# Query-key products of a causal attention regrouped by four PSUM banks and alternated between row halves

## The chip, the core and the metric

The kernel runs on one core of one Trainium2 chip. The metric is device time in microseconds (us) of that core; before the change the median of three runs was 1920.82 us (1916.88 to 1924.34). A core has engines with queues of their own that run side by side and wait for each other by semaphores: TensorE (PE: matrix products; its weight loads are listed apart as PEld), VectorE (DVE), ScalarE (ACT), GpSimd (POOL), and SyncE (SP), which here issues the DMAs. Products land in PSUM, which here is handed out in eight banks of 128 partitions x 512 fp32 values; VectorE and ScalarE read them from there.

## What is computed

One block of a hybrid model, on x of 4 x 256 x 512: attention with a rotary embedding and a small adapter prefix, a clustered feed-forward layer, a state-space mixer, and the feed-forward layer again, each added to x behind a layer norm. The change touches the attention alone:

```python
qkv = jnp.einsum('btc,oc->bto', x, w_attn)
...
q = _apply_rope(q, cos, sin)
k = _apply_rope(k, cos, sin)
scores = jnp.einsum('bhqd,bhkd->bhqk', q, k) / jnp.sqrt(jnp.asarray(hd, x.dtype))
causal = jnp.tril(jnp.ones((T, T), bool))
scores = jnp.where(causal, scores, jnp.asarray(-jnp.inf, x.dtype))
attn = jax.nn.softmax(scores, axis=-1)
y = jnp.einsum('bhqk,bhkd->bhqd', attn, v)
```

There are 32 heads of 16 values, 256 tokens in each of four sequences. Queries 0 to 127 can see keys 0 to 127 only; queries 128 to 255 see up to all 256.

## The kernel before, in words

`attention` goes through 32 units: four sequences of eight, a unit being four heads (`i` in the loop at L608). The steps of a unit are spread over four turns of that loop: `scores` of unit i, `turn` of unit i-1, `weigh` of i-2, `gathered` of i-3. Beside them run jobs in slices: `prepared` (norm and projections of the next sequence), `pieces` (rotated queries and keys stacked and transposed), `adapter_scores`, `adapted`, `ended` (output projection) and, in the last eight units, `fed` (feed-forward tiles).

The stacks made by `pieces` hold each head in 64 rows: the high and low parts of 16 values, in an order that makes one product of 64 rows the high-precision product of queries and keys. Two heads lie above each other in 128 partitions, so a head's product uses one half of TensorE's rows, `rows = slice(64 * pr, 64 * pr + 64)`.

`scores` (L413) works with four banks a unit: c is the block of 128 queries, pr the row half. For each bank it issues two products (L425, j = 0 and 1, always against all 256 keys), then a product of the identity with a mask (L429, all 128 rows, bf16), which adds -1e30 above the diagonal. VectorE takes the negative maximum (L434), ScalarE two exponentials with their sums (L437), one for each head in the bank; then the bank is free. `turn` (L443) transposes the exponentials in three tiles of four transposes (L452), each copied out (L453) by VectorE or ScalarE. `weigh` multiplies with the values (L462, L468), with four heads side by side in column strips of 32.

PSUM in this stage, eight banks: two under the tag "m" for everything general (`trp` L378, `pq` L269, `pa` L387, `pt` and `pya` in `adapted`, `try`, `po`, `pd`, `tr`), three for scores ("sc"), two for `turn` ("pt"), one for `weigh` ("py"). The projections of the first sequence (L359) and the last two feed-forward tiles (L660) borrow the score banks.

The order within each engine's queue isn't that of the source. A planner simulates the program, takes earlier instructions first but passes over those whose data or bank isn't ready, and fixes each queue before the run. In the queue of TensorE therefore stand transposes, products and pieces of other jobs between the banks of one unit.

## Time and profile before

| | |
|---|---|
| median of three runs | 1920.82 us |
| the profiled execution | 1916.66 us, span 1914.9 us |
| mean granted TensorE clock | 0.990 |
| products of L425 | 256, each 64 rows, 128 x 256 out; half of them for queries 0 to 127 |
| weight loads of L425 (min/median/max) | 182/184/336 ns |
| mask products of L429 | 128, weight loads 94/96/107 ns |
| maxima of L434 | 128, 359/550/693 ns |
| exponentials of L437 | 256, 356/446/534 ns, and as many sums of 185/203/264 ns |
| transposes of L452 | 384, and 96 copies of L453 of 680 (VectorE) or 587 ns (ScalarE) |

The span is the time from the first instruction to the last in one profiled execution; the time of that execution is longer by what lies around it. In lists of instructions the first number is the start in us from the start of the span, the second the length of the group; "x2" is the number merged into the line; the shape reads rows*columns of the weights, then the moving operand. In square brackets stands how long the engine was idle before and what ended the wait. "issue" is a wait that nothing in the profile explains. The ends of products are modelled, so two starts are a better measure of TensorE than one duration.

### The profile page before, as it was taken

The page shows a single profiled execution, that of the slowest core. Times are in us where ns is not written, and L with a number is a line of the kernel's source. Part 1 is how long each engine was busy: PE and PEld are TensorE (multiplying, and loading weights), DVE is VectorE, ACT ScalarE, POOL GpSimd, SP SyncE. Part 2 cuts the span into 40 slices and gives each one's busy share as a digit, 9 for nine tenths or more (in the row PEclk, how much of TensorE's full clock was granted, in tenths as well). Part 3 has the DMA queues.
Part 4 walks back from the last instruction along what each step waited for, and adds up shares of the span by engine and source line. Part 5 has one row for each costly group of instructions (what it writes and reads, how often), then busy time and mean ns, then how long its engine had stood idle before and what let it go on. Part 6 is the DMA issues. An engine that isn't in the chain of part 4 may idle for free.

```text
span 1914.9 us, 29954 instructions
## 1 busy us (share of the span) xinstructions
PE 1866.0 (97%) x10690; PEld 1468.9 (77%) x10690; DVE 1475.2 (77%) x2324; ACT 1383.2 (72%) x2873; POOL 361.0 (19%) x308
## 2 busy tenths in 40 slices
PE   7999999989999999999999999999999999999997
PEld 6767767767777787888787878877777788787786
DVE  5556657678998777877877797778777877877777
ACT  5665667557898677876787787778677877786753
POOL 4212120011331111222111121212111211131100
PEclk7999999989999999999999999999999999999999
DMA  4000000014455554544455454446454554455341
GB/s 141 1 1 1 1 21 24 12 38 155 169 192 184 160 168 140 160 154 160 149 164 161 149 172 156 148 147 187 149 165 154 160 159 160 138 166 162 119 123 49
DMA packets 151909, 240.35 MB, mean 126 GB/s; under 512 B 12368, under 2 KB 77520, under 8 KB 151760
## 3 DMA queue, kind: packets, MB, share of 16 engines
q1 hardware_dynamic: 151760, 238.44, 39.1%
q8 instruction: 84, 1.38, 0.3%
q14 instruction: 65, 0.53, 0.1%
HBM read 202.75 MB, written 35.65 MB: 124 GB/s over the span
## 4 chain that ended last, share of the span: by engine, by line
PE 84%; DVE 6%; ACT 4%; DMA 2%; issue 1%; SPq 0%; DVEq 0%; ACTq 0%
PE pp L112 12%; PE pp L113 11%; PE pp L114 11%; PE pyy L928 8%; PE pog L112 6%; PE pog L114 6%; PE pog L113 6%; PE sc L425 3%; PE trx L913 3%; PE ptr L452 2%; DVE acc L854 2%; PE py L462 1%; PE sc L429 1%; PE trp L380 1%; DMA wor<-in_wout_dram 1%
## 5 line engine op out<-in xcount | busy, mean ns | idle before, releaser
L112 PE MATMUL pp<-mx,w 128*128 128x512 f32 (+1 forms) x1160 | 465.6, 401 | 8.4 <-DVE acc L854 7.9
L114 PE MATMUL pp<-mx,w 128*128 128x512 f32 (+1 forms) x1160 | 454.2, 392 | 0.0
L113 PE MATMUL pp<-mx,w 128*128 128x512 f32 (+1 forms) x1160 | 454.2, 392 | 0.0
L854 DVE SCALAR_TENSOR_TENSOR acc<-pp,cw_s,acc 128x1012 f32<-128x1012 f32 (+2 forms) x240 | 304.8, 1270 | 23.1 <-ACT acc L847 22.4
L902 DVE TENSOR_TENSOR em<-em,gm 128x1536 f32<-128x1536 f32 x128 | 228.4, 1785 | 94.3 <-ACT em L896 86.0
L112 PEld LDWEIGHTS pp<-mx,w 128*128 128x128 f32 x1160 | 218.6, 188 | 66.0 <-issue 9.9
L114 PEld LDWEIGHTS pp<-mx,w 128*128 128x128 f32 x1160 | 218.5, 188 | 45.5 <-issue 0.4
L113 PEld LDWEIGHTS pp<-mx,w 128*128 128x128 f32 x1160 | 218.9, 189 | 40.7 <-issue 0.7
L890 POOL TENSOR_SCALAR_AFFINE_SELECT r<-r 128x512 f32<-128x512 f32 x128 | 144.6, 1129 | 526.6 <-DMA r<-cumd 418.5
L951 POOL TENSOR_TENSOR sq<-sq,acc 128x1024 f32<-128x1024 f32 x55 | 132.6, 2410 | 581.8 <-ACT acc L950 581.8
L104 ACT CAST w<-wr 128x512 fp32r<-128x512 f32 x144 | 88.5, 615 | 187.6 <-PE pp L113 164.4
L112 PE MATMUL pog<-wo,gh 128*128 128x512 f32 x512 | 204.3, 399 | 0.0
L114 PE MATMUL pog<-wo,gh 128*128 128x512 f32 x512 | 200.3, 392 | 0.0
L113 PE MATMUL pog<-wo,gh 128*128 128x512 f32 x512 | 199.9, 390 | 0.0
L895 ACT ACTIVATE em<-r,col_t 128x128 f32<-128x128 f32 x512 | 165.0, 391 | 48.2 <-PE pyy L928 46.5
L928 PE MATMUL pyy<-em,xd 128*64 128x256 f32 (+1 forms) x2048 | 189.1, 330 | 2.4 <-DVE em L902 2.4
L928 PEld LDWEIGHTS pyy<-em,xd 128*64 128x64 f32 x2048 | 134.2, 137 | 63.6 <-issue 21.7
L898 ACT ACTIVATE em<-r,col_t 128x128 f32<-128x128 f32 x512 | 166.5, 389 | 0.0
L886 DVE TENSOR_SCALAR em<-r,col_t 128x128 f32<-128x128 f32 x512 | 137.1, 327 | 12.1 <-PE pyy L928 10.1
L914 DVE TENSOR_TENSOR xd<-trx,dt_t 128x512 f32<-128x512 f32 x128 | 86.2, 683 | 54.6 <-PE trx L913 54.4
L105 DVE TENSOR_TENSOR w<-wr,w 128x512 fp32r<-128x512 f32 x139 | 97.4, 702 | 37.8 <-ACT w L104 37.3
L437 ACT ACTIVATE e<-sc,nmx 128x128 f32<-128x128 f32 (+1 forms) x256 | 105.2, 424 | 15.0 <-DVE nmx L434 14.9
(287 smaller groups left out, 3313.4 us busy)
## 6 DMA issues: line engine op xcount, KB each, us to landing
wr<-in_win_dram SPq DMA_DIRECT2D x287, 256.0 KB, 2.8
r<-cumd SPq DMA_DIRECT2D x128, 512.0 KB, 4.1
spill<-gb SPq DMA_DIRECT2D x63, 512.0 KB, 2.8
gr<-spill SPq DMA_DIRECT2D x120, 256.0 KB, 3.5
wor<-in_wout_dram SPq DMA_DIRECT2D x64, 256.0 KB, 3.1
out_dram<-x SPq DMA_DIRECT2D x8, 256.0 KB, 2.3
x<-in_x_dram SPq DMA_DIRECT2D x1, 1536.0 KB, 10.2
gr<-spill SPq DMA_DIRECT2D x8, 192.0 KB, 2.5
```

The costliest lines, as they stand in the source:

```text
L112: nc.tensor.matmul(o, lh, rh, start=(first and k == 0), stop=False)
L113: nc.tensor.matmul(o, lh, rl, start=False, stop=False)
L114: nc.tensor.matmul(o, ll, rh, start=False, stop=(last and k == n - 1))
L437: nc.scalar.activation(es_[c][:, 2 * j + pr, :], sc[:, j, :n], AF.Exp, bias=nm[:, j : j + 1], accum_out=rs[:, c, h : h + 1],)
L854: nc.vector.scalar_tensor_tensor(av[:, :, d:], pv[:, :, : L - d], cw_s[:, ch, tap : tap + 1], av[:, :, d:], ALU.mult, ALU.add,)
L886: nc.vector.tensor_scalar(e[:, b, 2, :], rv[:, b, 1, :], col_t[:, h, b, 1:2], 0.0, ALU.subtract, ALU.min,)
L890: nc.gpsimd.affine_select(rv[:, :, 0, :], rv[:, :, 0, :], pattern=[[0, B], [1, P]], compare_op=ALU.is_ge, fill=-1e30, base=0, channel_mult ...
L895: nc.scalar.activation(e[:, b, 1, :], rv[:, b, 1, :], AF.Exp, bias=col_t[:, h, b, 2:3])
L898: nc.scalar.activation(e[:, b, 0, :], rv[:, b, 0, :], AF.Exp, bias=col_t[:, h, b, 0:1])
L902: nc.vector.tensor_tensor(e, e, gm, ALU.mult)
L928: nc.tensor.matmul(py[d, b, k * P :], xd[:, 2 * b + k, d], es2[hh][:, b, 2 * k : 2 if k == 0 else 3, :].rearrange("p s i -> p (s i)"), sta ...
L951: (nc.gpsimd if n < NB - 1 else nc.vector).tensor_tensor(sq, sq, x2, ALU.add)
```

## The change

`scores` first issues the products of two banks of one query block in turn, upper half, lower half, upper, lower; the second query block (c = 1) comes before the first. For the first query block only keys 0 to 127 are multiplied (`kT[rows, blk, :n]`), and its tiles are half as wide. After all eight products come, bank by bank, mask, maximum and exponentials. The score pool has four banks; the transposition pool is gone and `turn` takes its tiles from the general pool, which has three.

```diff
-            ps = pool("a_m", 2, space=PSUM)
-            ps_s = pool("a_s", 3, space=PSUM)
-            ps_t = pool("a_t", 2, space=PSUM)
+            ps = pool("a_m", 3, space=PSUM)
+            ps_s = pool("a_s", 4, space=PSUM)
             ps_y = pool("a_y", 1, space=PSUM)
...
-                for c in range(2):
+                made = []
+                for c in (1, 0):
                     n = (c + 1) * P
-                    for pr in range(2):
-                        rows = slice(64 * pr, 64 * pr + 64)
-                        sc = ps_s.tile([P, 2, L], F32, name="sc", tag="sc")
-                        for j in range(2):
-                            blk = (u % 2) * 2 + j
+
+                    pair = [ps_s.tile([P, 2, n], F32, name="sc", tag="sc") for _ in range(2)]
+                    for j in range(2):
+                        blk = (u % 2) * 2 + j
+                        for pr in range(2):
+                            rows = slice(64 * pr, 64 * pr + 64)
                             nc.tensor.matmul(
-                                sc[:, j, :], qT[rows, blk, c * P : (c + 1) * P], kT[rows, blk, :],
-                                start=(j == 0), stop=False,
+                                pair[pr][:, j, :], qT[rows, blk, c * P : (c + 1) * P],
+                                kT[rows, blk, :n], start=(j == 0), stop=False,
                             )
-                        nc.tensor.matmul(
-                            sc[:, :, n - P : n], identb, negb.unsqueeze(1).to_broadcast([P, 2, P]),
-                            start=False, stop=True,
+                    made += [(c, pr, sc) for pr, sc in enumerate(pair)]
+                for c, pr, sc in made:
+                    n = (c + 1) * P
+                    nc.tensor.matmul(
+                        sc[:, :, n - P :], identb, negb.unsqueeze(1).to_broadcast([P, 2, P]),
+                        start=False, stop=True,
+                    )
+                    nm = p3.tile([P, 2], F32, name="nmx", tag="nmx", bufs=4)
+                    nc.vector.tensor_reduce(nm, sc, AX.X, ALU.max, negate=True)
+                    for j in range(2):
+                        h = 4 * u + 2 * j + pr
+                        nc.scalar.activation(
+                            es_[c][:, 2 * j + pr, :], sc[:, j, :], AF.Exp,
+                            bias=nm[:, j : j + 1], accum_out=rs[:, c, h : h + 1],
                         )
...
-                    pt = ps_t.tile([P, 4, P], F32, name="ptr", tag="pt")
+                    pt = ps.tile([P, 4, P], F32, name="ptr", tag="m")
```

The maxima get four small buffers instead of three. What the maxima and exponentials read is as wide as before.

More of the change, by code (lines that the diff above doesn't have):

```diff
@@ L425, in scores @@
                             nc.tensor.matmul(
-                                sc[:, j, :], qT[rows, blk, c * P : (c + 1) * P], kT[rows, blk, :],
-                                start=(j == 0), stop=False,
-                            )
-                        nc.tensor.matmul(
-                            sc[:, :, n - P : n], identb, negb.unsqueeze(1).to_broadcast([P, 2, P]),
-                            start=False, stop=True,
-                        )
-                        nm = p3.tile([P, 2], F32, name="nmx", tag="nmx")
@@ L434, in scores @@
-                        nc.vector.tensor_reduce(nm, sc[:, :, :n], AX.X, ALU.max, negate=True)
-                        for j in range(2):
-                            h = 4 * u + 2 * j + pr
-                            nc.scalar.activation(
-                                es_[c][:, 2 * j + pr, :], sc[:, j, :n], AF.Exp,
-                                bias=nm[:, j : j + 1], accum_out=rs[:, c, h : h + 1],
-                            )
+                                pair[pr][:, j, :], qT[rows, blk, c * P : (c + 1) * P],
```

## The prediction

> **What bounds the kernel now.** I read the engine totals and the 40 slices first, to see which engine is full and where.

> ```profile
> PE 1866.0 (97%) x10690; PEld 1468.9 (77%) x10690; DVE 1475.2 (77%) x2324; ACT 1383.2 (72%) x2873; POOL 361.0 (19%) x308
> ...
> PE   7999999989999999999999999999999999999997
> ...
> PEclk7999999989999999999999999999999999999999
> ```

> TensorE is busy in nearly every slice, at full clock. The changed functions run only in the attention stage, so I cut the trace in three: attention, the passage to the mixer, the mixer.

> ```profile
> core 0: us, PE busy (x) PEld busy (x) DVE busy (x) ACT busy (x) POOL busy (x), PEclk, DMA share, GB/s
> 36.00:370.00 334.00, 331.07 (x2288) 237.51 (x2288) 207.14 (x456) 217.35 (x775) 53.23 (x85) 0.98 0.03 8
> 370.00:440.00 70.00, 57.69 (x319) 47.34 (x318) 51.76 (x114) 36.21 (x60) 9.20 (x8) 0.93 0.15 45
> ```

> In the 334 us of attention VectorE is busy 62%, ScalarE 65%, the DMA engines 3%, TensorE 99%. A busy TensorE may still be stalled, since its ends are modelled; so I ask what waits for what at the line to be changed. TensorE's weight loads there wait 3.3 us in all for ScalarE's exponentials (L437) and 14.0 us for "issue" (64 times, some 0.2 us each), that is, for nothing but TensorE itself. The stage is bound by TensorE's own instruction stream, and time taken out of that stream should come off the span.

> What the stream costs at this place is in the timeline of TensorE alone (start, duration of the merged group, engine, line). Starts matter here, not durations: a product's record lasts some 0.28 to 0.38 us but the next one starts long before.

> ```profile
> 202.29 0.50 PE L425 MATMUL sc<-pc,pc 64*128 64x256 f32 x2
> 202.72 0.28 PE L429 MATMUL sc<-negb,identb 128*128 128x256 bf16 x1
> 202.94 0.50 PE L425 MATMUL sc<-pc,pc 64*128 64x256 f32 x2
> 203.37 0.28 PE L429 MATMUL sc<-negb,identb 128*128 128x256 bf16 x1
> 203.58 0.50 PE L425 MATMUL sc<-pc,pc 64*128 64x256 f32 x2
> 204.01 0.28 PE L429 MATMUL sc<-negb,identb 128*128 128x256 bf16 x1
> 204.13 0.30 PE L397 MATMUL tra<-con,sa 80*128 80x80 f32 x2
> ```

> Two products take 0.43 us until the mask product; the mask takes 0.12 us when a full-height instruction follows (204.01 to 204.13), and 0.21 when a half-height product follows (203.37 to 203.58). So going into half-height work costs 0.09 us. One score bank costs 0.09 + 0.43 + 0.12 = 0.64 us, a unit of four banks 2.57, the 32 units 82 us, a quarter of the stage. What would it cost if nothing were exposed? The nearest row is the adapter's score product, also 256 columns of the same type, but on all 128 rows. In the chain of waits (start, length of the piece):

> ```profile
> 201.51 0.50 PE pa L390 x4
> 202.01 0.35 PE py L468 x6
> 202.36 0.43 PE sc L425 x2
> 202.79 0.21 PE sc L429
> 203.01 0.43 PE sc L425 x2
> 203.44 0.22 PE sc L429
> ```

> Four of those take 0.50 us; start to start their median is 0.118. I use 0.12. Two products would thus need 0.24; the pair takes 0.43, so 0.19 is overhead: the first weight load, which nothing covers, and the emptying before the mask. With the entry, 0.28 us per bank goes to changing between half and full height. The whole chain of the page agrees that this is on the path:

> ```profile
> PE 84%; DVE 6%; ACT 4%; DMA 2%; issue 1%; SPq 0%; DVEq 0%; ACTq 0%
> PE pp L112 12%; PE pp L113 11%; PE pp L114 11%; PE pyy L928 8%; PE pog L112 6%; PE pog L114 6%; PE pog L113 6%; PE sc L425 3%; PE trx L913 3%; PE ptr L452 2%; DVE acc L854 2%; PE py L462 1%; PE sc L429 1%; PE trp L380 1%; DMA wor<-in_wout_dram 1%
> ```

> **The change, part by part.**

> *Grouping.* The eight products of a unit now stand in front of its four masks. If the four banks are free together, there is one entry and one exit instead of four: 0.28 + 8 x 0.12 + 4 x 0.12 = 1.72 us against 2.57, a saving of 0.85 us a unit, 27 us in all. How often are they free together? The order on TensorE is worked out beforehand by a planner that takes what is ready. Today the first three banks of a unit mostly go back to back, as above, and the fourth waits for a free bank. With four banks the same should hold for four. But some units follow within 4 us of each other, while a bank is freed only after its reduce (0.42 or 0.69 us) and two exponentials (starting 0.35 or 0.46 us apart, with their sums), 1.1 to 1.6 us for each bank in turn. Then the two pairs come apart, and each extra entry costs 0.28 us. I take one and a half entries a unit: 0.71 us, 23 us in all.

> *Alternation between the halves.* [...] Loads of 128 columns, one after the other, are 0.11 us each, which is the 0.12 that I already charge. [...]

> [...]

> *First queries take 128 keys, not 256.* Halves the columns of 128 products. At 0.11 us per load, a product of 0.06 us is hidden behind the next load: nothing. The reduce and the exponentials already read only n columns: no change on VectorE or ScalarE (70 and 158 us at these lines).

> *Order: second queries first, and masks later.* VectorE's first reduce of a unit waits for a mask behind up to eight products, 0.5 us later than now. Behind it in its queue stand copies that free transposition banks; VectorE has 38% idle, so it costs nothing unless TensorE is short of such a bank.

> *Banks.* Score banks 3 to 4; the general banks ("m", two) and the transposition banks ("pt", two) become three shared. I count some 210 general tiles and 96 transposition tiles in 334 us, 0.9 a microsecond. Three banks suffice if a tile holds one for 3.3 us on average. A rotated-piece tile holds it about 1.4 us (four transposes, copy of 0.68 or 0.59), a projection 4.3, but an attention transposition some 3, because its four transposes are issued as the exponentials come. That is two banks busy on average, so collisions happen, chiefly while `ended` or `fed` holds two. Bounds: below, a gain of 2 us, since general tiles may now use three banks; above, one exposed round of transposes and copy a unit, 0.44 + 0.68 + some 0.2 of handing over = 1.3 us, 42 us. Nearest row: TensorE's waits in the stage that end with a copy out of a shared or transposition bank (L380 and L452 behind L382, L453, L520; L479 behind L453 and L104; L163) add up to some 4 us. I take as much again: 4 us lost. No DMA is added or moved; what SP issues is the same.

> **Sum.** 23 - 4 = 19 us off. The profiled execution took 1916.66 us (span 1914.9 and 1.8 around it), so 1897.7; it lies 4.2 under the median of 1920.82, so the median should be 1902. What is late next in the stage is still TensorE; ScalarE goes from 65% to 217 / 315 = 69%. The passage behind attention is a chain of VectorE, ScalarE and TensorE steps anchored at attention's end and moves up as a whole.

> **Rivals.**

> *Halves run side by side* and the planner keeps the bursts whole: 27 + 15 - 4 = 38 us off, 1883. For it: concurrent column strips at L462. Against: their staggered loads.

> *The gain is not collected*: TensorE gets ahead and waits for exponentials or banks instead, within 9 us of now, about 1916. For it: each unit needs eight exponentials, 4 x 0.35 + 4 x 0.46 = 3.2 us of ScalarE, before its transposes can end. Against: a third of ScalarE and of VectorE is idle, and three units are in flight.

> *Slower: transposition tiles starve the shared banks.* Each of up to three transposition tiles of a unit holds a bank while it waits for exponentials, and the rotated pieces, adapter products and projections queue behind it on TensorE. At the upper bound of 42 us against 23 that is 19 us slower, 1940; it decides from 0.72 us of added stall a unit. For it: the 3 us holding time and the loss of the separate pool. Against: holdings average two of three. [...]

> **How the numbers follow.** Forecast 0.52, side by side 0.18, not collected 0.14, slower 0.16. A measurement of this kernel tells about 0.5% from no change, 9.6 us: the forecast's own range, 1890 to 1912, is almost all beyond it. Faster 0.70, same 0.15, slower 0.15. The range leaves out the best of the second case and the worst of the fourth: 1881 to 1930.

> **What would show it.** Right: runs of four or eight products with starts 0.11 to 0.12 us apart, one or two entries a unit, the attention stage some 19 us shorter, the mixer unchanged. Side by side: starts in pairs a few ns apart. Wrong: products 0.2 us or more apart within a run, or weight loads of transposes waiting for copies (L453, L382) for tens of microseconds.

## The result, and the profile after

The changed kernel took 1909.45 us (median of 20 runs, 1900.47 to 1923.63), the kernel before 1920.11 (20 runs, 1914.75 to 1924.34). The ratio is 0.9955, with a 95% interval of 0.9937 to 0.9974: some 9 us faster (the medians differ by 10.7), where 19 were forecast. Among all the runs below one stands apart, 5156.97 us in e9 without a known cause, and is left out of ratios and clocks. From the page of the changed kernel, engine totals and granted clock in 40 slices:

```profile
PE 1851.2 (97%) x10690; PEld 1465.2 (77%) x10690; DVE 1475.0 (77%) x2324; ACT 1380.2 (72%) x2873; POOL 352.4 (18%) x308
...
PEclk8999899989999999999999999999999999999999
```

and its three stages, with the same borders as before (busy time of each engine, then the granted clock):

```profile
36.00:370.00 334.00, 321.47 (x2318) 238.40 (x2316) 209.42 (x473) 215.86 (x778) 53.48 (x84) 0.96 0.03 9
370.00:440.00 70.00, 59.02 (x317) 47.81 (x317) 54.03 (x106) 40.62 (x65) 9.20 (x8) 0.93 0.16 52
440.00:1909.00 1469.00, 1444.04 (x7933) 1157.19 (x7931) 1187.56 (x1697) 1106.36 (x1996) 266.88 (x184) 1.00 0.48 155
```

The first pyy product of the mixer starts at 449.3 us instead of 456.6, 7.3 us earlier, and the span ends 6.1 us earlier (1908.8 against 1914.9); so all of the gain lies ahead of the mixer. The chain of waits over the whole span agrees:

```profile
PE 80%; DVE 8%; ACT 6%; DMA 3%; issue 2%; POOL 1%; SPq 0%; DVEq 0%; ACTq 0%; POOLq 0%
PE pp L112 12%; PE pp L113 11%; PE pp L114 11%; PE pyy L932 8%; PE pog L112 6%; PE pog L114 6%; PE pog L113 6%; PE trx L917 3%; DVE acc L858 2%; PE sc L426 1%; DMA wor<-in_wout_dram 1%; PE ptr L456 1%; ACT e L441 1%; PE trp L379 1%; PE py L466 1%
```

The products went from 3% to 1% of the chain, and TensorE from 84% to 80%; VectorE and ScalarE took over most of the difference, the exponentials among them (L441, not in the list before). In the window of attention TensorE isn't full any more (321 of 334 us), and its clock is 0.96 instead of 0.98. The products did become cheaper: added from each start to the next start on TensorE, they take 41.8 us instead of 58.8, while the masks behind them take 21.8 instead of 19.7. Together that is 14.9 us off TensorE's stream, where the forecast had 23. The timeline of TensorE shows both faces of the change, some 3 us apart (start, length of the group, line):

```profile
192.07 0.67 PE L426 MATMUL sc<-pc,pc 64*128 64x256 f32 x8
192.68 0.61 PE L433 MATMUL sc<-negb,identb 128*128 128x256 bf16 x4
...
194.87 0.50 PE L426 MATMUL sc<-pc,pc 64*128 64x256 f32 x2
195.30 0.28 PE L433 MATMUL sc<-negb,identb 128*128 128x256 bf16 x1
195.78 0.50 PE L426 MATMUL sc<-pc,pc 64*128 64x256 f32 x2 [0.20 <-ACT e L441]
...
196.69 0.32 PE L426 MATMUL sc<-pc,pc 64*128 64x128 f32 x1
196.94 0.87 PE L379 MATMUL trp<-con,st 128*128 128x128 f32 x8
197.74 0.32 PE L426 MATMUL sc<-pc,pc 64*128 64x128 f32 x1
198.00 0.53 PE L379 MATMUL trp<-con,st 128*128 128x128 f32 x4
```

At 192.07 a unit has its four banks together: eight products in 0.61 us until the mask; their starts are 0, 3, 221, 224, 339, 342, 397 and 401 ns. They start in pairs 3 or 4 ns apart: the two halves run beside each other. The rows don't name the halves, but the queue of the built kernel does. Of its 46 runs of two products, 15 hold one of each half, and the 14 in the order upper, lower start 3 or 4 ns apart; 31 hold one half only, and those start 162 ns or more apart. At 194.87 the next unit has to take its banks as ScalarE frees them ("<-ACT e L441"), and its products come in twos and ones. Over the stage there are 109 entries from other work into half-height products, against 136 before; runs of eight occur four times. TensorE's weight loads at the products wait 10.0 us for the exponentials, against 3.3. The clock falls behind some of these places. Two of them in the windows view, each row a stretch of 3.4 us or a multiple (length, busy time of the engines, and the clock in the third column from the end):

```profile
191.70:195.20 3.50, 3.26 (x31) 2.63 (x29) 2.13 (x5) 3.00 (x12) 0.92 (x2) 1.00 0.03 7
195.20:198.60 3.40, 3.20 (x23) 2.29 (x21) 2.93 (x6) 3.27 (x16) 0.46 (x1) 1.00 0.01 2
198.60:208.80 10.20, 10.20 (x54) 7.67 (x55) 4.44 (x10) 6.36 (x21) 0.14 (x1) 0.50 0.00 0
208.80:212.20 3.40, 3.26 (x27) 2.07 (x27) 2.17 (x6) 2.31 (x7) 1.50 (x3) 0.99 0.00 0
```

```profile
273.60:277.10 3.50, 3.38 (x34) 2.82 (x32) 1.52 (x4) 3.37 (x9) 1.30 (x3) 1.00 0.00 0
277.10:280.50 3.40, 2.18 (x12) 1.29 (x12) 2.95 (x6) 2.87 (x15) 0.00 (x0) 1.00 0.30 87
280.50:287.30 6.80, 6.80 (x37) 4.76 (x36) 4.63 (x8) 4.58 (x13) 1.24 (x3) 0.50 0.18 52
```

TensorE does 12 instructions between 277.1 and 280.5, among them a wait of 1.02 us for an exponential, and is busy 2.18 of 3.40 us; then it runs 6.8 us at half clock and is "busy" 100% of it, as in the 10.2 us from 198.6. So busy time alone misleads here: of these rows, the two at half clock are the busiest. From the start of the products to 370 us the kernel before has one half-clock stretch, 13.7 us from 35.0 on; the changed one has five, 3.4 us at 34.8, 6.8 at 45.0, 10.2 at 198.6, 6.8 at 280.5 and 3.4 at 355.6, together 30.6.

### The profile page after: what moved, and what is told of

The parts are those of the page before. It is cut to its first block, busy times and chain, and to the rows that moved or that the text cites. A ratio compares the mean times of both kernels' runs of the same rounds, so it can differ in the third digit from the quotient of the medians.

```text
span 1908.8 us, 29962 instructions
## 1 busy us (share of the span) xinstructions
PE 1851.2 (97%) x10690; PEld 1465.2 (77%) x10690; DVE 1475.0 (77%) x2324; ACT 1380.2 (72%) x2873; POOL 352.4 (18%) x308
## 4 chain that ended last, share of the span: by engine, by line
PE 80%; DVE 8%; ACT 6%; DMA 3%; issue 2%; POOL 1%; SPq 0%; DVEq 0%; ACTq 0%; POOLq 0%
PE pp L112 12%; PE pp L113 11%; PE pp L114 11%; PE pyy L932 8%; PE pog L112 6%; PE pog L114 6%; PE pog L113 6%; PE trx L917 3%; DVE acc L858 2%; PE sc L426 1%; DMA wor<-in_wout_dram 1%; PE ptr L456 1%; ACT e L441 1%; PE trp L379 1%; PE py L466 1%
## 5 line engine op out<-in xcount | busy, mean ns | idle before, releaser
L112 PE MATMUL pp<-mx,w 128*128 128x512 f32 (+1 forms) x1160 | 465.2, 401 | 8.7 <-DVE acc L858 8.2
L113 PE MATMUL pp<-mx,w 128*128 128x512 f32 (+1 forms) x1160 | 454.0, 391 | 0.0
L114 PE MATMUL pp<-mx,w 128*128 128x512 f32 (+1 forms) x1160 | 453.9, 391 | 0.0
L112 PEld LDWEIGHTS pp<-mx,w 128*128 128x128 f32 x1160 | 218.3, 188 | 66.4 <-issue 10.0
L114 PEld LDWEIGHTS pp<-mx,w 128*128 128x128 f32 x1160 | 218.6, 188 | 45.5 <-issue 0.4
L113 PEld LDWEIGHTS pp<-mx,w 128*128 128x128 f32 x1160 | 218.8, 189 | 40.7 <-issue 0.7
L894 POOL TENSOR_SCALAR_AFFINE_SELECT r<-r 128x512 f32<-128x512 f32 x128 | 135.3, 1057 | 539.7 <-DMA r<-cumd 399.6
L104 ACT CAST w<-wr 128x512 fp32r<-128x512 f32 x144 | 88.5, 615 | 189.5 <-PE pp L113 174.5
L112 PE MATMUL pog<-wo,gh 128*128 128x512 f32 x512 | 204.6, 400 | 0.0
L113 PE MATMUL pog<-wo,gh 128*128 128x512 f32 x512 | 200.1, 391 | 0.0
L114 PE MATMUL pog<-wo,gh 128*128 128x512 f32 x512 | 200.0, 391 | 0.0
L890 DVE TENSOR_SCALAR em<-r,col_t 128x128 f32<-128x128 f32 x512 | 137.5, 328 | 12.1 <-PE pyy L932 10.1
L441 ACT ACTIVATE e<-sc,nmx 128x256 f32<-128x256 f32 (+1 forms) x256 | 104.7, 434 | 13.1 <-DVE nmx L438 12.8
```

What stands on the lines that cost most here:

```text
L112: nc.tensor.matmul(o, lh, rh, start=(first and k == 0), stop=False)
L113: nc.tensor.matmul(o, lh, rl, start=False, stop=False)
L114: nc.tensor.matmul(o, ll, rh, start=False, stop=(last and k == n - 1))
L441: nc.scalar.activation(es_[c][:, 2 * j + pr, :], sc[:, j, :], AF.Exp, bias=nm[:, j : j + 1], accum_out=rs[:, c, h : h + 1],)
L890: nc.vector.tensor_scalar(e[:, b, 2, :], rv[:, b, 1, :], col_t[:, h, b, 1:2], 0.0, ALU.subtract, ALU.min,)
L894: nc.gpsimd.affine_select(rv[:, :, 0, :], rv[:, :, 0, :], pattern=[[0, B], [1, P]], compare_op=ALU.is_ge, fill=-1e30, base=0, channel_mult ...
```

## The experiments

The first theory (A): the saving is there, and is given back through waits for score banks and the half clock that follows them. Its rival (B): the shared general banks starve the transposes, which the forecast priced at 4 us. All ratios are to the kernel before, run beside it; it isn't exactly the quotient of two medians. The clock is the mean over the whole span and the runs.

| kernel | us | ratio, 95% interval | clock |
|---|---|---|---|
| the change | 1909.45 | 0.9955, 0.9937 to 0.9974 | 0.9855 |
| e1_pools_only | 1924.63 | 1.0028, 1.0016 to 1.0039 | 0.9887 |
| e2_old_banks | 1900.63 | 0.9902, 0.9888 to 0.9916 | 0.9878 |
| e3_all_keys | 1905.81 | 0.9930, 0.9918 to 0.9941 | 0.9906 |
| e4_no_alternation | 1908.89 | 0.9950, 0.9935 to 0.9964 | 0.9878 |
| e5_old_banks_all_keys | 1903.68 | 0.9919, 0.9906 to 0.9932 | 0.9890 |
| e6_halved_keys_only | 1915.39 | 0.9979, 0.9972 to 0.9987 | 0.9892 |
| e7_pairs | 1905.43 | 0.9926, 0.9914 to 0.9939 | 0.9883 |
| e8_three_score_banks | 1906.97 | 0.9933, 0.9915 to 0.9952 | 0.9908 |
| e9_mask_twice | 1916.86 | 0.9982, 0.9975 to 0.9988 | 0.9921 |
| e10_turn_first | 1917.81 | 0.9982, 0.9970 to 0.9993 | 0.9863 |
| e11_two_bank_tiles | 1912.25 | 0.9964, 0.9950 to 0.9977 | 0.9902 |
| e12_four_two_one | 1900.68 | 0.9909, 0.9894 to 0.9923 | 0.9892 |

The kernel before had a mean clock of 0.9892 in the 71 runs beside e1 to e12.

**The banks alone, and without them.** To the kernel before:

```diff
-            ps = pool("a_m", 2, space=PSUM)
-            ps_s = pool("a_s", 3, space=PSUM)
-            ps_t = pool("a_t", 2, space=PSUM)
+            ps = pool("a_m", 3, space=PSUM)
+            ps_s = pool("a_s", 4, space=PSUM)
...
-                    pt = ps_t.tile([P, 4, P], F32, name="ptr", tag="pt")
+                    pt = ps.tile([P, 4, P], F32, name="ptr", tag="m")
```

> The kernel before with the change's banks alone (three shared general banks, four score banks); products as before. Theory A (the saving is there, and is given back through waits for score banks and half-clock stretches of TensorE that follow): about the time before, 1915 to 1922, clock as before (0.99), with products still near 59 us of TensorE. Theory B (the shared banks starve the transposes): 6 to 12 us slower than before, with weight loads of transposes and general tiles waiting for copies.

The reverse of that diff, on the changed kernel:

> The changed kernel with the banks of before (two general, three score, two for transposes). Theory A: three score banks cannot hold a unit's two pairs, so fewer pairs side by side; products some 45 to 50 us instead of 42; time between before and after, about 1910 to 1915, clock no better than after. Theory B: the sharing was the loss, so about 1900, faster than after by 8 or more.

With the products untouched the new banks cost 5.4 us (0.0028 x 1919) at an unchanged clock. Without them the changed products gain 0.0098, 18.8 us, against 8.6 with them. So B has the sign right on both kernels, and A was wrong on both. The size is less sure: on the kernel before, the interval runs from 3 to 7.5 us, which holds the forecast's 4; on the changed products the same exchange is worth 10.2. What waits is in the view of the transposition tile in the changed kernel, "who waited for it" (us, times):

```profile
  PEld try L483: 2.1, 6
  PE pt L513: 1.7, 2
  PEld pq L112: 1.2, 3
  PEld ptr L456: 0.8, 2
```

Those are general tiles waiting behind transposition tiles, 5 us in all; in the kernel before the same view names one of them, `try`, with 1.0 us. In e1 it has 1.2 us for `try` and 0.8 for `pt`, so the waits seen explain less than half of its 5.4; the rest isn't shown.

**Is it the fourth score bank, the number of the others, or the sharing?**

```diff
# e8, to the change
-            ps_s = pool("a_s", 4, space=PSUM)
+            ps_s = pool("a_s", 3, space=PSUM)
# e12, to the change
-            ps = pool("a_m", 3, space=PSUM)
+            ps = pool("a_m", 2, space=PSUM)
+            ps_t = pool("a_t", 1, space=PSUM)
...
-                    pt = ps.tile([P, 4, P], F32, name="ptr", tag="m")
+                    pt = ps_t.tile([P, 4, P], F32, name="ptr", tag="pt")
```

> The changed kernel with three score banks instead of four, the three general banks still shared with the transposes, one bank unused. If the sharing is what costs (bank theory), as slow as the change or slower, 1909 to 1916. If the fourth score bank costs, because it lets the scores run ahead of ScalarE, near e2_old_banks, 1900 to 1904.

> The changed kernel with four score banks, two general banks and a single one of its own for the transposes. If the sharing (transposes holding general banks) is what costs 5 us: about 1904. If the number of banks outside the scores (three instead of four) costs, however they are divided: 1909 or slower, up to 1925, since three transposition tiles a unit take turns in one bank.

e12 has the same eight banks as the change, only divided: two general and one for the transposes. It is 8.8 us faster than the change and as fast as e2 with its 2 + 2. So three banks beside the scores suffice, and the sharing is what costs (in part by way of the clock, see below). The transposes then wait for their own bank, and this holds up hardly anybody else's tile:

```profile
  PEld ptr L457: 6.0, 17
  PE ptr L457: 0.4, 2
  PEld pd L114: 0.4, 1
```

e8 fits neither of its readings: it lies between, 6 us behind e2, from which it differs only in the sharing (and one bank fewer).

**The halved keys.** `kT[rows, blk, :n]` became `kT[rows, blk, :]` again, with full tiles, once on the change and once on e2; and the cut alone was made in the kernel before.

> The changed kernel, but the first queries multiply all 256 keys again. Each of 64 pairs of such products costs 0.055 us more at TensorE, 3.5 us in all. Theory A with the halved products as what lets the clock fall: clock back to 0.99 and 1902 to 1908. Theory A with the waits as what lets it fall: clock as after (0.978 to 0.992 from run to run) and 1909 to 1914. Theory B: 1913.

> The changed products with the banks of before, and all 256 keys for the first queries. [...] Bank theory (the clock has nothing to do with the columns): 3.5 us slower than e2_old_banks, about 1904.

The clock theory of the next one is e3's reading in which the halved products let the clock fall:

> The kernel before, with only the first queries' products cut to 128 keys. The forecast said nothing is gained since loads bound; taken for the pair as it stands before, 64 banks lose at most 0.055 us each, so 3.5 us: about 1916 at equal clock. Clock theory: mean clock some 0.001 to 0.003 lower than the kernel before, 2 to 5 us given back, so 1916 to 1921. Bank theory: 1916, clock unchanged.

With separate transposition banks the cut is worth 3.1 us (e5 against e2, whose intervals overlap), alone 4.0 us (e6), both at about the same clock (0.9878 against 0.9890; 0.9892 with and without the cut). On the change as it stands it is worth less than nothing: all keys are 3.6 us faster, with the clock at 0.9906 instead of 0.9855. That is the reading of e3 in which the halved products let the clock fall. But e5's bank reading (1904) came true, at nearly e2's clock: with the old banks the cut hardly touches it. So halved products go with a lower clock at most where the banks are shared, and not always there (e8 has 0.9908).

**Order and grouping.** e4 exchanges the loops over j and pr, so that a bank's two products come one after the other.

> The changed kernel, products grouped but first both of the upper half, then both of the lower. If the forecast was right that the weight loads bound a run of products whatever the half, the same time as after (1909) and products near 42 us. If the halves do run side by side, pairs no longer coincide and products cost 8 to 12 us more, so 1915 to 1920 at equal clock.

The time doesn't change. In TensorE's queue of e4, as the kernel is built, the products of a run of eight stand two of the upper half, two of the lower, and so on; in the change they alternate. The timeline of e4:

```profile
196.67 0.68 PE L426 MATMUL sc<-pc,pc 64*128 64x256 f32 x8
197.28 0.61 PE L433 MATMUL sc<-negb,identb 128*128 128x256 bf16 x4
```

The same 0.61 us for eight products as with alternation, with starts at 0, 7, 220, 230, 342, 348, 402 and 404 ns. The first two in the queue are of one half, and such a pair alone starts 162 ns or more apart; so the product 7 ns behind the first must be one of the lower half, which starts ahead of an upper one that stands before it. So in e4 as in the change, both halves of the array work side by side where products for both stand near each other in the queue (eight in 0.61 us); alternating them is worth nothing measurable (0.9950 and 0.9955, intervals overlap; products 43.3 us instead of 41.8). Both of my readings of e4 were wrong in their reasoning; the number of the first came true.

e7 puts masks, maxima and exponentials after each pair of banks, on e2's banks:

```diff
-                    made += [(c, pr, sc) for pr, sc in enumerate(pair)]
-                for c, pr, sc in made:
-                    n = (c + 1) * P
+                    for pr, sc in enumerate(pair):
```

> The changed products with the banks of before, and the masks after each pair of banks instead of after all four. If grouping by four banks carries the gain (forecast: 0.28 us an entry), some 32 more entries, 6 to 9 us slower than e2_old_banks, about 1908. If the gain is the two halves running beside each other within a pair, and the planner splits the groups anyway, the same as e2_old_banks, 1897 to 1904.

120 entries instead of 111, and 4.8 us slower than e2: between the two readings, and 9 more entries where 32 were expected. e11 forces whole pairs:

```diff
-            ps_s = pool("a_s", 4, space=PSUM)
+            ps_s = pool("a_s", 2, space=PSUM)
...
-                    pair = [ps_s.tile([P, 2, n], F32, name="sc", tag="sc") for _ in range(2)]
+                    both = ps_s.tile([P, 2, 512], F32, name="sc", tag="sc")
+                    pair = [both[:, v, : 2 * n].rearrange("p (j k) -> p j k", j=2) for v in range(2)]
```

> The changed kernel, but a pair of score banks is one tile of two banks, given out and freed together: four products of a pair can only be issued together. Entries into half-height work at most 64 instead of 109; at 0.28 us each (the forecast's price) 12 us less TensorE work: 1897 to 1903 if that was the missing part of the grouping. But a bank waits for both exponential pairs to be free: if waits for score banks take its place, 1908 to 1920.

Entries fall to 91 and the products to 34.2 us, the least of all kernels; yet the time is 1912.25. The stage's line shows where it went, TensorE busy 309 of 334 us at a clock no worse than before:

```profile
36.00:370.00 334.00, 309.19 (x2308) 225.50 (x2306) 207.97 (x467) 216.42 (x776) 52.22 (x83) 0.98 0.03 9
```

Grouping by force exchanges TensorE work for TensorE waits, the second reading. In the list of who waits for the tile `sc`, TensorE's masks now wait 7.3 us and VectorE's maxima 34.9, against 14.1 in the change. e10 moves `turn` ahead of `scores` in the loop at L608, on e2's banks:

> The changed products with the banks of before (e2_old_banks), and the transposes of the last unit ahead of the scores of this one in the source, so that the planner prefers them. If TensorE's waits for score banks (10 us in e2_old_banks) come from scores put too early: waits down to a few us, clock up, 1893 to 1898. If the planner's order hardly moves: 1899 to 1903.

A miss in the other direction: 17 us slower than e2, with the waits at the products for exponentials up from 9.8 to 14.2 us in the weight loads. The copies of the transposes wait 59.9 us for TensorE instead of 14.6. So scores put later in the source aren't better; why the planner's order comes out so much worse stays open.

**The clock.** The change's 20 runs are the same program, and differ in their clock and time together: 1901.39 us at 0.992, 1922.88 and 1923.63 at 0.978. A line through all 20 falls by 16.4 us for each 0.01 of clock, with a correlation of -0.96. At the 0.9892 of the kernel before, it gives 1904.6 us. By this line the other 4.8 us of the median (6 of the mean) go with the clock. e9 tries this from outside: it issues each mask product twice (the second adds to entries that the exponential makes zero anyway), so that the stage has more full-height work.

> The changed kernel with every mask product issued twice, the first time as filler: 128 full-height products of 256 columns more, 128 x 0.12 = 15 us of TensorE work. Clock theory (a 3.4 us stretch in which the array is used little halves the clock of the next): full-height filler in the unit keeps the clock up, mean 0.990 to 0.993 with little spread, so about 1909 + 15 - 6 to 10 = 1914 to 1918. If the waits alone trip the clock: clock as in the change (0.9855), 1921 to 1926.

The clock rises to 0.9921, and the 20 runs draw together, 1915.2 to 1920.4, as the clock theory said. The masks take 12.1 us more of TensorE (33.9 against 21.8), the median rises by 7.4. So the clock stays up with full-height filler, which seems to pay back a good third of its own time; the order in the queue changes with it (122 entries instead of 109), so the filler isn't proved to be the only cause. It isn't a way to speed: 1916.86 is still behind the change.

What in the change brings the clock down is no single part of it. Sharing with all keys (e3) has 0.9906, sharing with three score banks (e8) 0.9908, halved keys on banks of their own (e2, e6, e12) 0.9878 to 0.9892; only the change itself and e10's order lie under 0.987. So it seems to depend on the order that the planner makes of the whole, and what decides in it stays open. As an estimate by the slope of that line, the sharing costs 2 us (the change against e12) to 5 us (against e2, and e3 against e5) at equal clock; of the 8.8 us between the change and e12 some 6 go with the clock.

How little work stands ahead of a fall of the clock can be read from the traces. In those of both kernels every stretch of the granted clock in attention lasts 3.41 us or a multiple of it (3.41, 6.83, 10.24, 13.65 and longer). I cut each trace into steps of 3.41 us along these stretches and added up, for the products starting in a step at full clock, columns x share of the array's 128 rows x share of its 128 columns. For comparison: products of 512 columns on 128 rows and 128 columns start 227 ns apart where they follow each other (median, before and after alike), which makes some 7700 columns a step. In the 14 traces, from 36 to 370 us: of 25 steps under 1802 columns (0.23 of that), 20 were followed by half clock; of 24 between 1802 and 2130 (0.28), 5; of 1246 above, 4. The step at 195.2 above is one of these four: 94% busy by the profile, with 2752 columns (0.36). So the measure is a rough one, and why that step was followed by half clock stays open.

## Why the prediction was wrong

- **What bounds the stage**: right before the change. After it, TensorE's own stream is no longer alone; the waits that the forecast's third case named ("the gain is not collected") took a share.
- **Grouping, 23 us**: e5 (old banks and all keys) measures 15.5 us (0.0081 x 1919) for the regrouped products, and its trace agrees: products and masks take 62.8 us of TensorE instead of 78.5. The count of entries was wrong: one and a half a unit are 48, the planner left 107 in e5 and 109 in the change, where banks come free one by one (as at 194.87). The 15.5 us hold what the halves gain side by side; no run separates the two. Nor does one separate the 0.19 us that I put down to a pair's first load and to the emptying before the mask: the load is in the rows (182 ns at the least), the emptying was my estimate.
- **Alternation, no term in the sum**: the size is right, the argument wrong. I took loads of the two halves to follow one another, from the column strips of the value product. But I had read a rare spacing there: of the 201 spacings under 60 ns between loads of L462, 23 are near 27 ns and 157 under 10 (median 7). The same timeline of the kernel before has eight of them, of about 0.11 us each, in 0.16 us:

```profile
200.21 0.16 PEld L462 LDWEIGHTS py<-eT,av 128*32 128x32 f32 x8
```

Read so, that row too, whose products start 5 to 8 ns apart, spoke for the halves running side by side, and they do: pairs start 3 ns apart (the sign that the forecast named for that rival), 118 ns for a pair of 256 columns. The 15 us in the rival's sum were my estimate, a unit's eight products in 4 x 0.12 us instead of 8 x 0.12, 32 times; no run shows that term, only the 0.61 us for eight, from the first start to the mask, in runs of eight that occur four times in the stage. But the alternation isn't needed for it (e4). My 0.12 us for a product was therefore double its cost in a run, which made up for part of the missing groups; that is luck.

- **Halved keys, nothing**: 3 to 4 us (e6, e2 against e5). A short product was not hidden behind the next load: in e6, where a bank's two products have no partner in the other half, they start 164 ns apart with 128 columns and 223 with 256. The 59 ns, 64 times, are 3.8 us.
- **Banks, 4 us lost**: 5.4 (e1), and 2 to 5 at equal clock in the changed kernel; the direction is as written and the size about right. The mechanism, general tiles behind transposition tiles, shows in 5 us of waits in the change, but not in all of e1's loss.
- **No term for the clock**: the failed step. "TensorE is busy in nearly every slice, at full clock" was taken over for the time after, and a fall of the clock was priced at nothing. The runs show a mean of 0.9855 instead of 0.9892, and the line through the 20 runs puts 5 to 6 us on it. At equal clock the parts give 15.5 + 4.0 - 5.4 = 14 us, and the line says 15. What is left of the forecast's 19 is a second, smaller miss: grouping was 7.5 us too large, and the 3 to 4 us of the halved keys, put at nothing, made up for half of that. The sign was right.

The version to keep is e2 or e12: the changed products, and banks for the transposes that are theirs alone. Both gain twice what the change gains, and are faster than both kernels.

## What to carry to other kernels

When work is taken from a TensorE-bound stage, look at what the engine does with the time: here TensorE was busy 321 instead of 331 of 334 us in attention, its mean clock over the span fell from 0.9892 to 0.9855, and with it went 5 to 6 us of the saving (in e11, busy 309 us, the clock was 0.9902). Give a long-held tile its own PSUM banks rather than a larger shared pool: the same eight banks, divided otherwise, were worth 9 us here, some 6 of them with the clock. And count how often the planner can form a group, from how banks come free, before a price per group is multiplied.
